# Expert stages of a fused transformer-and-state-space kernel: the slot tiles behind the sixteenth in nested conditional blocks

## The chip, the core and the metric

The kernel runs on one core of a Trainium2 chip. A core has five engines, each with its own instruction queue and its own sequencer: TensorE (PE: matrix products and transposes; its weight loads are listed as PEld), VectorE (DVE), ScalarE (ACT), GpSimd (POOL) and SyncE (SP, which here only issues transfers). Sixteen DMA engines move data between HBM and the on-chip memory. ACT, SP and POOL issue transfers. Engines wait for each other through semaphores.

The metric is the device time of one execution in microseconds (us). Before the change it is 2927.6 us, the median of three runs (2926.86 to 2928.7).

## The reference

One sequence of 1024 tokens of width 512 passes through two layers. Each part adds to the residual stream x:

```python
x = x + 0.5 * _L0_ffn_ref(_layernorm(x), ...)     # f0: 8 experts, top 2
x = x + _L0_attn_ref(_layernorm(x), ...)          # attention, 32 heads
x = x + 0.5 * _L0_ffn_ref(_layernorm(x), ...)     # f1: the same experts again
x = x + 0.5 * _L1_ffn_ref(_layernorm(x), ...)     # product with low-rank experts
x = x + _L1_attn_ref(_layernorm(x), ...)          # Mamba-like scan, 64 heads
x = x + 0.5 * _L1_ffn_ref(_layernorm(x), ...)
```

The part that the change touches is the first feed-forward network, which stands twice:

```python
logits = x @ W_gate + b_gate
_, top_idx = jax.lax.top_k(logits, 2)
y_all = jax.nn.relu(jnp.einsum('bsd,edh->bseh', x, W_e) + b_e)
y = jnp.take_along_axis(y_all, top_idx[..., None], axis=2)
return y.mean(axis=2)
```

Each token needs the outputs of two of eight experts, so 2048 rows in all go through some expert's 512x512 matrix.

## The kernel before

**The expert stage.** `expert_ffn(tag, ...)` runs twice, as f0 at the start and as f1 after the attention. It doesn't compute all eight experts for every token. It sorts the 2048 token-expert pairs into *slots*: each expert gets a whole number of tiles of 128 rows, at least one. The number of tiles in use depends on the data and lies between 16 (all counts multiples of 128) and 23. The program is laid out for the most, `NS = 2*S//P + NE - 1 = 23`, and always runs all 23. A tile behind the last one in use gathers token 0, multiplies it by the last expert's matrix, and stores rows that nobody reads.

**Routing.** VectorE computes from the gate's logits the two chosen experts of each token, the number of tiles of each expert (`nt`) and its running sum (`ends`; its last column is the number of tiles in use), the slot of each pair (`slot`), the token of each slot (`token`) and the expert of each tile (`of_i`).

**One slot tile** s then takes these steps.
- `gather(s)`: POOL issues an indirect transfer of 128 rows of the normalized input from the HBM buffer `rows` into a tile `xs` (three buffers).
- `turn(s)`: TensorE transposes it in four pieces (`ps_tr`, the helper's line L156), ACT copies the result to `xt_s` (three buffers, L494).
- Four products of 128x512 (`ps_e`, L527) with the expert's matrix, which is picked from `w_all` by a register that TensorE's sequencer loads from `of_i` (L523). Each product takes two passes.
- VectorE adds the expert's bias (`y_e`, L535, picked by a register of its own), ACT applies the relu and the factor 0.25 (L541) and issues the store of the tile to the HBM buffer `outs` (L542).

The loop runs one step ahead: `turn(s+1)` stands in front of the product of tile s, and gathers are issued two tiles ahead. A scheduler orders each engine's instructions at build time and places the waits.

**Work put between tiles.** `meanwhile` is a list of closures, one of which is run after every second tile from the fifth on. In f0 these load the first attention weights (`w_v`, `w_q`, `w_k`, `w_o`, SP queue) and then scale w_q (L676) and form sums of w_q and w_k on POOL (L653) for the first group of heads. In f1 they load and prepare weights of the second layer.

**Around the stage.** Before it, SP loads `w_all` (8 MB) and `b_all`. In f0 the first normalized tiles use a pool `own` of five buffers that is released after them. Behind it, `collect` issues two indirect gathers per token tile on POOL (`pair<-outs`, L555), VectorE adds them to x (L572), and a layer norm and the next stage's first products follow, tile by tile. The first collecting gather needs all stores to `outs`.

Of the kernel before, what the change touches and what calls it, by code (L numbers as in the profile page):

```python
# [13 lines left out]
F32 = mybir.dt.float32  # L14
BF16 = mybir.dt.bfloat16
I32 = mybir.dt.int32
# [6 lines left out]
P = 128  # L23
S = 1024
D = 512
NT = S // P
KT = D // P
# [6 lines left out]

NE = 8
NS = 2 * S // P + NE - 1
NE1 = 4
RANK = 8

# [36 lines left out]
def macaron_kernel(  # L76
# [23 lines left out]
    nc = tc.nc  # L100
# [8 lines left out]
    rows = dram.tile([S, D], F32, tag="rows", name="rows")  # L109
    outs = dram.tile([NS * P, D], F32, tag="outs", name="outs")  # L110

# [6 lines left out]
    x = const.tile([P, NT, D], F32, tag="x", name="x")  # L118
# [40 lines left out]
    def normalize(t, keep=False, pin=False, own=None):  # L159

        st = lnp.tile([P, 6], F32, tag="st", name="ln_st")
        nc.vector.bn_stats(st, x[:, t, :])
        mv = lnp.tile([P, 2], F32, tag="mv", name="ln_mv")
        nc.vector.bn_aggr(mv, st)
        rs = lnp.tile([P, 1], F32, tag="rs", name="ln_rs")
        root = rsqrt(rs, mv[:, 1:2], 1.0, EPS, 1)
        if pin:
            tc.keep_in_program_order(root)
        if own is None:
            xn = lnp.tile([P, D], F32, tag="xn", name="ln_xn")  # L170
        else:
            xn = own.tile([P, D], F32, tag="own", name="xn_own")
        nc.vector.tensor_scalar(xn, x[:, t, :], mv[:, 0:1], rs, ALU.subtract, ALU.mult)
        if keep:
            nc.scalar.dma_start(rows[t * P : (t + 1) * P, :], xn)
        normal[t] = xn
# [19 lines left out]
    def narrow_by_columns(t, w, n):  # L196

        ps = psml.tile([P, 512], F32, tag="ps", name="ps_nc")  # L200
        for k in range(KT):
            nc.tensor.matmul(
                ps[(k % 2) * MP : (k % 2) * MP + n, :P],
                lhsT=w[:, k, :n],
                rhs=hT[:, k, t * P : (t + 1) * P],
                start=(k < 2),
                stop=True,
                skip_group_check=k >= 2,
            )
        nt = halves[t % 2]  # L210
        if n == MP:
            nc.scalar.copy(nt, ps[:, :P])
        else:
            for i in range(2):
                nc.scalar.copy(nt[i * MP : i * MP + n, :], ps[i * MP : i * MP + n, :P])
        narrow[t] = nt
# [89 lines left out]
    def gate_steps(own=None):  # L306
        return (
            lambda t: normalize(t, True, own=own),
            transpose_h,
            None,  # L310
            lambda t: narrow_by_columns(t, gate_w, NE),
            gates,
        )

    def expert_ffn(tag, before_rows, meanwhile, behind_weights=lambda: None):
# [4 lines left out]

        with tc.tile_pool(name=f"{tag}wa", bufs=1) as wap, tc.tile_pool(
            name=f"{tag}r", bufs=1
        ) as rp, tc.tile_pool(name=f"{tag}w", bufs=3) as wk:
            w_all = wap.tile([P, NE, KT, D], F32, tag="w_all", name="w_all")
            b_all = wap.tile([P, NE, D], F32, tag="b_all", name="b_all")
            for e in range(NE):
# [3 lines left out]
                if e % 4 == 3:  # L330
                    for b in range(e - 3, e + 1):
                        nc.sync.dma_start(b_all[:, b, :], b_e[b].partition_broadcast(P))
            behind_weights()


            lanes = rp.tile([P, P], F32, tag="lanes", name="lanes")
            steps = rp.tile([P, NS + 1], F32, tag="steps", name="steps")
            counts = rp.tile([P, P], I32, tag="counts", name="counts")
            nc.gpsimd.iota(counts, pattern=[[1, P]], base=0, channel_multiplier=0)
            nc.gpsimd.tensor_copy(lanes, counts)  # L340
            nc.gpsimd.tensor_scalar(steps, lanes[:, : NS + 1], float(P), None, ALU.mult)
            lane = rp.tile([P, 1], F32, tag="lane", name="lane")
# [11 lines left out]
            nc.gpsimd.memset(going_on, 1.0)  # L354
            nc.gpsimd.memset(going_on[:, :, 0:1], 0.0)

            before_rows()
            sel1 = first_of_max(rp, lg, NE, "a")
            rest = rp.tile([P, NT, NE], F32, tag="rest", name="rest")
            nc.vector.scalar_tensor_tensor(rest, sel1, -3e38, lg, ALU.mult, ALU.add)  # L360
# [45 lines left out]
            ends = rp.tile([P, NE], F32, tag="ends", name="ends")  # L406
# [15 lines left out]
            for i, sel in enumerate((sel1, sel2)):  # L422
# [7 lines left out]
            flat = pos.rearrange("p i t -> p (i t)")  # L430
            past = rp.tile([P, n2, NS + 1], F32, tag="past", name="past_s")
            nc.vector.tensor_tensor(
                past,
                flat.unsqueeze(2).to_broadcast([P, n2, NS + 1]),
                steps.unsqueeze(1).to_broadcast([P, n2, NS + 1]),
                ALU.is_ge,
# [39 lines left out]
            gathered, turned = {}, {}  # L476

            def gather(s):
                xs = wk.tile([P, D], F32, tag="xs", name="xs")
                nc.gpsimd.indirect_dma_start(  # L480
                    out=xs,
                    out_offset=None,
                    in_=rows,
                    in_offset=bass.IndirectOffsetOnAxis(ap=token[:, s : s + 1], axis=0),
                    bounds_check=S - 1,
                    oob_is_err=True,
                )
                gathered[s] = xs

            def turn(s):  # L490
                xs = gathered.pop(s)
                ps = transposes(lambda i: xs[:, i * P : (i + 1) * P], KT)
                xt = wk.tile([P, KT, P], F32, tag="xt", name="xt_s")
                nc.scalar.copy(xt.rearrange("p k c -> p (k c)"), ps)  # L494
                turned[s] = xt

# [16 lines left out]
            for i in range(2):  # L513
                nc.vector.tensor_copy(slot[i], pos[:, i, :])
            turn(0)
            for s in range(NS):
                if s + 2 < NS:
                    gather(s + 2)
                if s + 1 < NS:
                    turn(s + 1)  # L520
                xt = turned.pop(s)
                low, high = max(0, s - (NS - NE)), min(s, NE - 1)
                ep = nc.tensor.value_load(of_i[0:1, s : s + 1], min_val=low, max_val=high)  # L523
                ev = nc.vector.value_load(of_i[0:1, s : s + 1], min_val=low, max_val=high)
                ps = psml.tile([P, 512], F32, tag="ps", name="ps_e")
                for k in range(KT):
                    nc.tensor.matmul(  # L527
                        ps,
                        lhsT=xt[:, k, :],
                        rhs=w_all[:, bass.ds(ep, 1), k, :].rearrange("p e c -> p (e c)"),  # L530
                        start=(k == 0),
                        stop=(k == KT - 1),
                    )
                y = wk.tile([P, D], F32, tag="y", name="y_e")
                nc.vector.tensor_tensor(  # L535
                    y,
                    ps,
                    b_all[:, bass.ds(ev, 1), :].rearrange("p e c -> p (e c)"),
                    ALU.add,
                )  # L540
                nc.scalar.activation(y, y, AF.Relu, scale=0.25)  # L541
                nc.scalar.dma_start(outs[s * P : (s + 1) * P, :], y)  # L542
                if s > 3 and s % 2 == 0 and meanwhile:
                    meanwhile.pop(0)()

    pairs = {}

# [27 lines left out]
    class Lora:  # L575


        def __init__(self, pool):
            self.store = False
            self.pool = pool  # L580
            self.nz = NE1 * RANK
            self.lg_w = pool.tile([P, KT, self.nz + NE1], F32, tag="lg_w", name="lg_w")
            nc.scalar.dma_start(self.lg_w, lora_gate_t.rearrange("(k p) c -> p k c", p=P))
            self.lb_w = pool.tile([self.nz, D], F32, tag="lb_w", name="lb_w")
            nc.scalar.dma_start(self.lb_w, lora_b)
            self.ebias = pool.tile([P, NE1], F32, tag="ebias", name="ebias")
            nc.scalar.dma_start(self.ebias, exp_bias.partition_broadcast(P))
# [5 lines left out]
        def gate(self, t):  # L593
            narrow_by_columns(t, self.lg_w, self.nz + NE1)

        def choose(self, t):
            nz = self.nz
            ps = narrow_by_rows(t, nz + NE1)
            lg = self.pool.tile([P, 1, NE1], F32, tag="lg", name="lg1")
            nc.vector.tensor_tensor(lg[:, 0, :], ps[:, nz : nz + NE1], self.ebias, ALU.add)  # L600
# [822 lines left out]
    with tc.tile_pool(name="left", bufs=1) as left:  # L1423
        first, later = {}, []
        causal = left.tile([P, P], F32, tag="causal", name="causal")
        make_causal_mask(nc, causal, mask_val=-1e30)

        def load_first():
            first.update(load_heads(0))
            first["left"] = left_of_heads(first, left, later)  # L1430

        later.append(load_first)

        def gates_of_input():
            with tc.tile_pool(name="own", bufs=5) as own:
                Tiles(*gate_steps(own)).flush()

        expert_ffn("f0", gates_of_input, later)
        attention(left, causal, first, Tiles(*gate_steps()))
    with tc.tile_pool(name="lora", bufs=1) as lp:  # L1440
        lora, par = Lora(lp), Scan(lp)
        expert_ffn("f1", lambda: None, [lora.load, par.ready, par.turn], par.load)
        mamba(lora, par)


# [49 lines left out]
```

## Time and profile before

| | |
|---|---|
| median of three runs | 2927.6 us |
| the profiled execution | 2928.29 us, of which its span 2926.6 us |
| granted TensorE clock, mean | 0.976 |
| f0: loop of slot tiles | first product 55.7 us, last pass ends 147.0 us |
| f1: loop of slot tiles | first product 1635.5 us, last pass ends 1725.8 us |
| products of both loops | 368 passes, 168.0 us busy |

The stretches around both loops, with the busy time of each engine, the granted clock of TensorE and the share of the DMA engines, read

```
0.00:46.50 46.50, 18.76 (x131) 12.41 (x131) 22.93 (x93) 9.97 (x25) 9.25 (x41) 0.80 0.98 346
46.50:60.00 13.50, 6.28 (x16) 3.45 (x17) 0.00 (x0) 1.17 (x2) 7.86 (x6) 0.57 0.88 288
60.00:147.10 87.10, 85.48 (x262) 41.51 (x260) 15.21 (x22) 24.14 (x43) 30.91 (x24) 1.00 0.42 124
147.10:187.00 39.90, 19.90 (x55) 10.02 (x56) 20.96 (x48) 5.13 (x10) 22.63 (x24) 0.70 0.39 112
1634.00:1726.00 92.00, 91.74 (x277) 44.95 (x275) 15.37 (x23) 25.50 (x46) 20.26 (x20) 0.98 0.42 122
```

(stretch and its length, then PE, PEld, VectorE, ACT and POOL busy us with the number of instructions, the granted clock, the DMA share and GB/s). In the profile, a line gives the engine, the source line, the operation with the tiles that it writes and reads, and in square brackets how long the engine had been idle and what ended that. "PEld", "PEq" or "PEldq" mark weight loads and TensorE's sequencer. In the chain of waits each piece is the work, or the wait, that the next one needed.

### The profile page before, as it was taken

The page shows a single profiled execution, that of the slowest core. Times are in us where ns is not written, and L with a number is a line of the kernel's source. Part 1 is how long each engine was busy: PE and PEld are TensorE (multiplying, and loading weights), DVE is VectorE, ACT ScalarE, POOL GpSimd, SP SyncE. Part 2 cuts the span into 40 slices and gives each one's busy share as a digit, 9 for nine tenths or more (in the row PEclk, how much of TensorE's full clock was granted, in tenths as well). Part 3 has the DMA queues.
Part 4 walks back from the last instruction along what each step waited for, and adds up shares of the span by engine and source line. Part 5 has one row for each costly group of instructions (what it writes and reads, how often), then busy time and mean ns, then how long its engine had stood idle before and what let it go on. Part 6 is the DMA issues. An engine that isn't in the chain of part 4 may idle for free.

```text
span 2926.6 us, 30414 instructions
## 1 busy us (share of the span) xinstructions
PE 2785.7 (95%) x11091; PEld 1578.9 (54%) x11091; DVE 1746.5 (60%) x3239; ACT 718.8 (25%) x1414; POOL 899.2 (31%) x737
## 2 busy tenths in 40 slices
PE   5979999999999999999999769899999999999998
PEld 3435666656666566666655334455555555555554
DVE  3146556565555655556555235677676777777673
ACT  2212212222212222212222223422222232222221
POOL 4231212121121211212200230255555545555451
PEclk7989999999999999999999889999999999999999
DMA  8421001010010001000015340233232222323210
GB/s 291 128 77 29 15 15 44 1 44 15 15 44 15 29 15 31 28 15 29 15 36 189 97 131 16 86 101 104 79 120 90 91 80 101 108 87 108 101 44 29
DMA packets 102180, 197.02 MB, mean 67 GB/s; under 512 B 9040, under 2 KB 34800, under 8 KB 102032
## 3 DMA queue, kind: packets, MB, share of 16 engines
q1 hardware_dynamic: 84896, 157.15, 16.3%
q0 software_dynamic: 6240, 20.45, 2.7%
q10 hardware_dynamic: 10896, 17.47, 1.6%
q8 instruction: 90, 1.47, 0.2%
q14 instruction: 58, 0.48, 0.1%
HBM read 176.17 MB, written 18.87 MB: 67 GB/s over the span
## 4 chain that ended last, share of the span: by engine, by line
PE 84%; DVE 6%; POOL 4%; DMA 3%; issue 3%; ACT 0%; SPq 0%; POOLq 0%; DVEq 0%; ACTq 0%
PE ps_in L247 15%; PE ps_m L929 13%; PE ps_o L749 8%; PE ps_s L725 8%; PE ps_tr L156 6%; PE ps_m L901 6%; PE ps_out L1377 6%; PE ps_wo L838 6%; PE ps_e L527 5%; PE ps_y L1325 3%; PE ps_up L258 2%; PE ps_st L1343 1%; DVE e_seg L1282 1%; DVE xc L1178 1%; PE ps_v L258 1%
## 5 line engine op out<-in xcount | busy, mean ns | idle before, releaser
L725 PE MATMUL ps_s<-kT,qT 128*128 128x512 f32 (+3 forms) x768 | 292.8, 488 | 0.1
L749 PE MATMUL ps_o<-pT,v 128*128 128x512 f32 (+3 forms) x768 | 258.6, 486 | 0.2 <-ACT pT L770 0.2
L770 ACT COPY pT<-ps_tr 128x256 f32<-128x256 f32 (+2 forms) x192 | 91.7, 477 | 646.5 <-PE ps_tr L156 635.0
L739 ACT ACTIVATE pr<-ps_s,nm 128x128 f32<-128x128 f32 (+7 forms) x256 | 190.3, 744 | 238.9 <-DVE nm L736 208.4
L1377 PE MATMUL ps_out<-w_out,yg 128*128 128x512 f32 x512 | 237.2, 606 | 2.0 <-DVE yg L1340 2.0
L247 PE MATMUL ps_in<-hT,w_g 128*128 128x512 f32 x512 | 226.7, 596 | 12.0 <-issue 12.0
L1307 POOL TENSOR_TENSOR cs<-cT,dd 128x1024 f32<-128x1024 f32 x56 | 181.7, 3245 | 163.8 <-PE ps_y L1325 139.4
L247 PE MATMUL ps_in<-hT,w_x 128*128 128x512 f32 x512 | 225.9, 593 | 0.0
L749 PEld LDWEIGHTS ps_o<-pT,v 128*128 128x128 f32 x768 | 143.5, 190 | 144.7 <-issue 98.8
L736 DVE TENSOR_REDUCE nm<-ps_s 128x1 f32<-128x128 f32 (+7 forms) x256 | 192.4, 753 | 3.9
L156 PEld LDWEIGHTS ps_tr<-ident,pr 128*128 128x128 f32 x1152 | 136.2, 141 | 76.4 <-issue 44.9
L156 PE MATMUL ps_tr<-ident,pr 128*128 128x128 f32 x1152 | 170.6, 275 | 4.4 <-DVE pr L741 3.2
L741 DVE TENSOR_SCALAR pr<-pr,sm 128x128 f32<-128x128 f32 (+7 forms) x256 | 163.8, 640 | 7.7 <-DVE sm L740 0.5
L527 PE MATMUL ps_e<-w_all,xt_s 128*128 (+1 forms) x368 | 168.0, 601 | 0.0
L247 PEld LDWEIGHTS ps_in<-hT,w_g 128*128 128x128 f32 x512 | 96.7, 190 | 132.1 <-issue 132.0
L247 PEld LDWEIGHTS ps_in<-hT,w_x 128*128 128x128 f32 x512 | 96.9, 190 | 120.4 <-issue 119.7
L1282 DVE TENSOR_TENSOR_SCAN e_seg<-dd,eye 128x1024 f32<-128x1024 f32 x64 | 153.9, 2404 | 8.2 <-PE ps_y L1325 6.1
L1178 DVE SCALAR_TENSOR_TENSOR xc<-ps_in,conv,xc 128x511 f32<-128x511 f32 (+2 forms) x192 | 141.6, 738 | 18.0 <-ACT xc L1174 17.6
L725 PEld LDWEIGHTS ps_s<-kT,qT 128*128 128x128 f32 x768 | 127.5, 192 | 39.8 <-issue 26.8
L1377 PEld LDWEIGHTS ps_out<-w_out,yg 128*128 128x128 f32 x512 | 93.0, 192 | 95.0 <-issue 94.6
L1301 POOL TENSOR_TENSOR xw<-xdt,erev 128x512 f32<-128x512 f32 x56 | 59.4, 1061 | 254.7 <-DVE xdt L1295 224.4
L823 POOL TENSOR_TENSOR so<-oT 128x256 f32<-128x256 f32 x28 | 20.1, 727 | 380.1 <-DVE oT L756 336.7
(274 smaller groups left out, 4760.5 us busy)
## 6 DMA issues: line engine op xcount, KB each, us to landing
dd<-decay SPq DMA_DIRECT2D x128, 512.0 KB
w_all<-in_w_e_dram SPq DMA_DIRECT2D x16, 1024.0 KB
outs<-y_e ACTq DMA_DIRECT2D x46, 256.0 KB
w_v<-in_wkv_dram SPq DMA_DIRECT2D x8, 1024.0 KB
w_q<-in_wq_dram SPq DMA_DIRECT2D x32, 256.0 KB
w_k<-in_wkv_dram SPq DMA_DIRECT2D x8, 1024.0 KB
w_o<-in_wo_dram SPq DMA_DIRECT2D x8, 1024.0 KB
w_x<-in_in_wt_dram SPq DMA_DIRECT2D x8, 1024.0 KB
```

What stands on the lines that cost most here:

```text
L156: nc.tensor.transpose(ps[:, i * P : (i + 1) * P], src(i), ident)
L247: nc.tensor.matmul(ps[:, cols : cols + n], lhsT=w[:, k, c0 : c0 + P], rhs=hT[:, k, t0 : t0 + n], start=(k == 0), stop=(k == KT - 1),)
L527: nc.tensor.matmul(ps, lhsT=xt[:, k, :], rhs=w_all[:, bass.ds(ep, 1), k, :].rearrange("p e c -> p (e c)"), start=(k == 0), stop=(k == KT - 1),
L725: nc.tensor.matmul(ps[:, j : j + m], lhsT=qT[:, qt * P : (qt + 1) * P], rhs=kT[:, j : j + m], start=True, stop=True,)
L736: nc.vector.tensor_reduce(nm, ps[:, :n], AX.X, ALU.max, negate=True)
L739: nc.scalar.activation(pr[:, :n], ps[:, :n], AF.Exp, bias=nm, accum_out=sm)
L749: nc.tensor.matmul(ps[:, lo:512], lhsT=v[:, kb, hh * P : (hh + 1) * P], rhs=pT[:, kb, lo:512], start=(kb == 0), stop=(kb == last),)
L838: nc.tensor.matmul(ps[:, j, :], lhsT=lf[i][k][:, j * P : (j + 1) * P], rhs=rt[i][:, k, :], start=(first and j == 0 and k == 0), stop=(k == 1),
L929: nc.tensor.matmul(ps, lhsT=gr["left"][i][:, k, hh * P : (hh + 1) * P], rhs=right[i][:, k, :], start=(first and k == 0), stop=(last and k ...
L1282: nc.vector.tensor_tensor_scan(e.rearrange("p h l -> p (h l)"), dd[:, 0, :], eye8.rearrange("p h l -> p (h l)"), 0.0, ALU.mult, ALU.add,)
L1307: nc.gpsimd.tensor_tensor(cs, un["cT"][:, tok].unsqueeze(1).to_broadcast([P, HPG, P]), dd[:, 1, :].rearrange("p (h l) -> p h l", l=P), ALU ...
L1377: nc.tensor.matmul(po, lhsT=yg[:, k, :], rhs=w_o[:, k, :], start=(k == 0), stop=(k == 3))
```

## The change

Tiles 0 to 15 run as before. Tiles 16 to 22 stand each inside a conditional block, and the blocks are nested: block s is entered if the number of tiles in use, n, is larger than s. When it is not, everything inside, so all later tiles, is left out. Four engines (PE, DVE, ACT and SP) load n into a register and compare it at each block; POOL has no instruction inside the blocks. In the built order each engine's blocks follow on one another, each opened by a compare-and-branch; the else parts and their jumps stand behind the last block. An else part waits for its engine's own work and brings its semaphores, and for SP those of the skipped stores, to the values that the skipped instructions would have left.

Five other things change with it.
- All gathers are issued outside the blocks. Those of tiles 16 to 18 use `xs` as before; those of 19 to 22 use a pool `more_rows` of five buffers, the one that held f0's first normalized tiles, which is now kept for the whole stage. In the built order of POOL these four stand right behind the gathers of tiles 2 to 4, and in f0 the scaling of w_q now stands behind the gather of tile 5.
- For tiles 16 and later the transposed rows are copied back into the gathered tile, not into `xt_s`.
- The register loads of `of_i` for tiles 16 to 22 stand inside the blocks.
- The work left in `meanwhile` is done before the first block.
- In f0 SP writes seven tiles of x to the rows of `outs` that belong to tiles 16 to 22, ahead of the attention weights. These rows then hold defined values also where no block stores.

```diff
+NS0 = 2 * S // P
...
             behind_weights()
+            if tag == "f0":
+                nc.sync.dma_start(
+                    outs[NS0 * P :, :].rearrange("(s p) c -> p s c", p=P), x[:, : NS - NS0, :]
+                )
...
             def gather(s):
-                xs = wk.tile([P, D], F32, tag="xs", name="xs")
+                if s < NS0 + 3:
+                    xs = wk.tile([P, D], F32, tag="xs", name="xs")
+                else:
+                    xs = more_rows.tile([P, D], F32, tag="own", name="xs_m")
...
             def turn(s):
...
-                xt = wk.tile([P, KT, P], F32, tag="xt", name="xt_s")
+                if s < NS0:
+                    xt = wk.tile([P, KT, P], F32, tag="xt", name="xt_s")
+                else:
+                    xt = xs.rearrange("p (k c) -> p k c", c=P)
...
             turn(0)
-            for s in range(NS):
-                if s + 2 < NS:
-                    gather(s + 2)
+            n_i = rp.tile([P, 1], I32, tag="n_i", name="n_i")
+            nc.vector.tensor_copy(n_i, ends[:, NE - 1 :])
+
+            def slot_tile(s):
                 if s + 1 < NS:
                     turn(s + 1)
...
                 nc.scalar.dma_start(outs[s * P : (s + 1) * P, :], y)
-                if s > 3 and s % 2 == 0 and meanwhile:
+
+            for s in range(NS0):
+                for i in range(s + 2, NS if s == NS0 - 2 else min(s + 3, NS)):
+                    if i not in gathered and i > 1:
+                        gather(i)
+                slot_tile(s)
+                if (s > 3 and s % 2 == 0) and meanwhile:
                     meanwhile.pop(0)()
+            while meanwhile:
+                meanwhile.pop(0)()
+
+            with ExitStack() as more_tiles:
+                n = nc.values_load(
+                    n_i[0:1, :],
+                    engines=[mybir.EngineType.PE, mybir.EngineType.DVE, mybir.EngineType.Activation, mybir.EngineType.SP],
+                    min_val=NS0,
+                    max_val=NS,
+                )
+                for s in range(NS0, NS):
+                    more_tiles.enter_context(tc.If(n > s))
+                    slot_tile(s)
```

More of the change, by code (lines that the diff above doesn't have):

```diff
@@ L322, in expert_ffn @@
             name=f"{tag}r", bufs=1
-        ) as rp, tc.tile_pool(name=f"{tag}w", bufs=3) as wk:
+        ) as rp, tc.tile_pool(name=f"{tag}m", bufs=5) as more_rows, tc.tile_pool(name=f"{tag}w", bufs=3) as wk:
             w_all = wap.tile([P, NE, KT, D], F32, tag="w_all", name="w_all")
@@ L355, in expert_ffn @@
             nc.gpsimd.memset(going_on[:, :, 0:1], 0.0)
-            before_rows()
+            before_rows(more_rows)
             sel1 = first_of_max(rp, lg, NE, "a")
@@ L1432, in macaron_kernel, with gates_of_input @@
         later.append(load_first)
-        def gates_of_input():
-            with tc.tile_pool(name="own", bufs=5) as own:
-                Tiles(*gate_steps(own)).flush()
+        def gates_of_input(own):
+            Tiles(*gate_steps(own)).flush()
         expert_ffn("f0", gates_of_input, later)
@@ L1441, in macaron_kernel @@
         lora, par = Lora(lp), Scan(lp)
-        expert_ffn("f1", lambda: None, [lora.load, par.ready, par.turn], par.load)
+        expert_ffn("f1", lambda own: None, [lora.load, par.ready, par.turn], par.load)
         mamba(lora, par)
```

## The prediction

> **What bounds the kernel now.** I read the page first, then the chain of waits around the first expert stage (0 to 200 us), then the timeline of both stages by engine, then the rows of single tiles. The two expert stages (called f0 and f1 in the code) are the only places that the change touches: after I take away buffer numbers and line numbers, the built order of the changed kernel has the same instructions in the same order on every engine outside them.
>
> ```profile
> span 2926.6 us, 30414 instructions
> PE 2785.7 (95%) x11091; PEld 1578.9 (54%) x11091; DVE 1746.5 (60%) x3239; ACT 718.8 (25%) x1414; POOL 899.2 (31%) x737
> L527 PE MATMUL ps_e<-w_all,xt_s 128*128 (+1 forms) x368 | 168.0, 601 | 0.0
> ```
>
> TensorE is busy for 95% of the span, and the expert product (L527) runs 368 times: two stages of 23 slot tiles, 8 passes each. It never waits (0.0).
>
> ```profile
> 135.83 0.44 PE ps_tr L156 x4
> 136.27 3.44 PE ps_e L527 x8
> 139.70 0.44 PE ps_tr L156 x4
> 140.14 6.88 PE ps_e L527 x16
> 147.10 0.70 DVE y_e L535
> 147.83 0.64 ACT y_e L541
> 148.49 2.00 DMA outs<-y_e
> 150.55 0.49 issue
> 151.26 0.34 POOL pair L555
> ```
>
> This is the chain of waits in f0 (start, duration, engine, tile, line). A slot tile costs the chain 0.44 + 3.44 = 3.87 us, all TensorE: the four transposes of the next tile, then this tile's eight passes. The last tile has no transposes to make and costs 3.44. Behind it stands a tail that any last tile leaves: bias on VectorE, relu, the store, its landing, the first collecting gather, 4.2 us from 147.02 to 151.26. f1 has the same period, and its first collecting gather starts 4.4 us after its last pass (1725.75 to 1730.19). So what is taken off the number of tiles comes off the span at TensorE's price, if nothing else becomes late.
>
> ```profile
> L527 PEldq EVENT_SEMAPHORE  x46: 51/51/3560, 54.8 to 1715.4; - x46
> L523 PEldq TENSOR_LOAD <-of_i x23: 295/299/812, 1621.2 to 1716.1; - x23
> 1714.66 0.69 DVE L535 TENSOR_TENSOR y_e<-ps_e,b_all 128x512 f32<-128x512 f32 x1 [3.18 <-PE ps_e L527]
> 1718.71 7.03 PE L527 MATMUL ps_e<-w_all,xt_s 128*128 x16
> ```
>
> These are rows of TensorE's sequencer (the first from the product's line, the second from the tile of_i in f1; durations are min/median/max) and two of f1's timeline. The sequencer waits at 1715.4 for VectorE's y of two tiles ago (1714.66 + 0.69), then issues a whole tile in 0.7 us (its next row, a register load for the last tile, is at 1716.1), while the array starts that tile at 1718.71. It is 3.3 us ahead of the array. And the register loads of f1 stand between its tiles (the built order has the last five there), where the period is still 3.87 us: one load costs the array nothing.
>
> **The change part by part.** I evaluated the reference's routing on its own inputs (seed 0). The counts per expert are 248 221 241 282 295 279 237 245 in f0, which makes 19 tiles of 128 in use, and 269 225 255 258 296 258 225 262 in f1, which makes 21. So 4 and 2 of the 23 tiles are skipped.
>
> *Removed.* f0: three tiles of 3.87 and the last one's 3.44, 15.05 us; f1: 3.87 + 3.44 = 7.31 us. Together -22.4 us. The transposes of the first unused tile (19 in f0, 21 in f1) are still made in the block before, and are counted in its 3.87.
>
> *The blocks.* f0 runs three blocks and leaves at the fourth compare; f1 runs five and leaves at the sixth. In each, TensorE's sequencer gets a compare and a register load of of_i with two register operations (before they were mostly done ahead of the loop). The load is 0.30 us by its row; the compare has no row. The nearest are the register operations (0.05 us each), so 0.4 to 0.5 us per block; the lead of 3.3 us hides it, and without that lead 8 blocks would cost 8 x 0.5 = 4 us. VectorE idles 3.18 us per tile and ScalarE 2.76, which hides theirs. Value taken 0; bounds 0 and +4. [...]
>
> *The exits.* Each engine jumps to an else part that waits for its own work and adds what the skipped tiles would have added to its semaphores. Behind it, TensorE's first work waits 16.5 us anyway (transposes at 163.48), ScalarE's 16.2 us, VectorE's 6.9 us. SyncE adds for the skipped stores: it waits for older stores of the same semaphores (by the built order none younger than tile 14's in f0), so it is through before the last store lands. POOL's first gather now waits also for TensorE's addition, which comes 4 us before the landing. I take 0.5 us per stage, +1.0; bounds 0 and, if each exit cost as much as a whole DMA round (2.0 us, the row of the store), +4.
>
> *The fill.* In f0 SyncE writes 7 tiles of x (1.84 MB) to the unused rows of outs, behind the last bias row and ahead of w_v, w_q, w_k, w_o. By the DMA view of 20 to 70 us the engines are full and move about 390 GB/s until 55, so this is 1.84 / 0.39 = 4.7 us of their time. Late next is not a weight (w_v is used at 169, w_q is scaled at 56 before and later now) but the first gathers: the one issued at 46.78 is transposed at 53.72, 6.9 us later; in f1, with idle DMA, 1628.89 to 1633.61, 4.7 us. If the queues share, the gather is slowed no more than now (0); if the backlog is served in order, by the bytes that stand ahead. Each transfer waits for the one eight before it, so the fill replaces w_k in what is outstanding at 46.8: 0.79 MB more, 2 us. Bounds 0 and +4.7, value +1.5.
>
> *POOL's order.* The gathers of tiles 19 to 22 now stand early (two behind the third gather, in the 4.4 us that POOL idles at 50.7; one each behind the next two), and the scaling of w_q moves behind the sixth gather. Now there is a stall in f0:
>
> ```profile
> 71.51 2.36 POOL L653 TENSOR_TENSOR sqk<-w_q,sqk 128x1024 f32<-128x1024 f32 x1
> 74.03 1.04 POOL L480 DMA_INDIRECT xs<-rows,token  x1 [0.16 <-issue]
> 77.55 0.63 PE L156 MATMUL ps_tr<-ident,xs 128*128 128x128 f32 x4 [1.53 <-DMA xs<-rows,token]
> ```
>
> Three sums hold the seventh gather until 74.03, and its rows come 1.53 us late. In the new order that gather stands behind two scalings (2 x 2.78) after the sixth (61.3 + 1.1): it issues at about 68.0, needs 3.5 us, and is there well before 75.9. The eighth stands behind three sums: 68.0 + 1.1 + 3 x 2.36 = 76.2, there at 79.7, needed at 79.75. So the stall shrinks to 0 to 0.5. Value -1.2; bounds -1.5 and +1.
>
> *Sum* against the profiled execution (2928.3 us, span 2926.6): 2928.3 - 22.4 + 0 + 1.0 + 1.5 - 1.2 = 2907.2. It lies 0.7 above the median of the runs (2927.6), so 2906.5 to 2907.2; I say 2907.
>
> **The rivals.**
>
> *Every compare fetches instructions.* The page's instruction queue q8 moved 1.47 MB in 90 packets, 0.2% of 16 engines' span: 0.002 x 16 x 2926.6 / 90 = 1.0 us a packet; with a round like the store's 2.0 us a fetch is about 3 us. TensorE's lead of 3.3 us just covers it. ScalarE does 0.59 + 0.63 + 0.33 = 1.55 us of a tile's 3.87; 3.0 more makes 4.55, so 8 blocks lose 0.7 each, 5.5 us, and the exits (two jumps in f0, three in f1, on VectorE against 6.9) 9.0 - 6.9 = 2.1. Time 2907 + 7.6 = 2915. For it: nothing here has ever branched inside the program. Against it: a used block follows straight on in the built order, and the jump is over some 130 instructions at most. [...]
>
> *The lead is lost*: the sequencer can't run ahead over a compare, and each block pays its loads, the four issues and the first weight load with an idle array, about 1 us by the 0.7 us that issuing a tile takes and the 0.3 of the load: 8 x 1 = 8, 2915 too.
>
> *Slower: each block is a barrier.* If a block starts only when the tile before has been stored, as the stage's end does, it pays the tail of 4.2 us: 8 x 4.2 = 34, so 2907 + 34 = 2941. It decides from 22.4 / 8 = 2.8 us per block. For it: at the stage's end just this wait is seen. Against it: the built order shows no barrier at a compare, its waits there are on the routing's count alone, and the next tile's transposes still stand ahead of a tile's product.
>
> *The gain is given back at the start*: fill served wholly first and the gathers behind it, +4.7, with the stall kept (+1.2) and exits at +4, blocks +4: 2907 + 3.2 + 1.2 + 3 + 4 = 2918, still faster.
>
> *It doesn't skip as counted*: another rounding on the chip moves a count over 256 (f1 has 255 and 258): 3.87 us either way, 2903 or 2911; it is held in the forecast's own range.
>
> **How the numbers follow.** Forecast as summed (2903 to 2911) 0.71; fetches or lost lead (2911 to 2918) 0.13; start and exits at their bounds 0.04; barrier 0.07; another cost of branches that just eats the gain, with no place that I can name, 0.05. The range 2903 to 2917 leaves out the barrier, the nameless cost and the ends of the rest. About 0.2%, 5.9 us, is what a measurement of this kernel can tell from no change, so faster means below 2921.7: 0.71 + 0.13 + 0.04 = 0.88; same 0.05; slower 0.07.
>
> **What would show it.** Right: the product's line with 184 + 184 - 48 = 320 passes; 19 and 21 tiles at a period of 3.87 us through the 17th and later; 4.2 to 5 us from the last pass to the first collecting gather; f0's first product within 0 to 3 us of 55.7; the stall at the seventh tile gone. Wrong: gaps of TensorE in front of each tile from the 17th (lead lost above 0.5 us, fetch on ScalarE if y waits there, barrier at 4 us); VectorE's first sum in x later than 7.6 us behind the last y; the first product of f0 later than 59; or 368 passes.

## The result, and the profile after

The changed kernel takes 2904.7 us, the median of five runs (2902.9 to 2907.5), against 2927.6 us for the kernel before (five runs, 2925.7 to 2930.5). The ratio is 0.9921, with a 95% interval of 0.9907 to 0.9936. The change makes the kernel faster by 22.9 us; 2907 was predicted. The profiled execution has a span of 2903.0 us at a granted clock of 0.977, so in the two profiles the span is shorter by 23.6 us.

From the page of the changed kernel, the busy times:

```profile
PE 2761.5 (95%) x11027; PEld 1567.6 (54%) x11027; DVE 1741.1 (60%) x3235; ACT 713.1 (25%) x1404; POOL 898.6 (31%) x737
```

TensorE is busy for 24.2 us less (2785.7 to 2761.5), which is the whole gain and a little more. It executes 64 matrix instructions fewer: six tiles of eight passes, 48, and four transposes for each of four tiles. (Tiles 19 and 21 are still turned, by the block ahead of them.) The queue that carries instructions moves as many packets as before, 90. The rows of the product's line, now L540, say the same:

```profile
L540 PE MATMUL ps_e<-w_all,xt_s x256: 592/592/1061, 55.6 to 1681.9; 128*128 x120, 128*128 128x512 f32 x8
L540 PE MATMUL ps_e<-w_all,xs x48: 592/592/595, 120.4 to 1693.5; 128*128 x48
L540 PE MATMUL ps_e<-w_all,xs_m x16: 592/592/595, 1694.4 to 1701.3; 128*128 x16
```

256 + 48 + 16 passes make 320 in place of 368. The columns behind the count are the shortest, median and longest duration in ns and the first and last start in us. The last two `xs_m` tiles are those of f1, whose 20th and 21st tile stand in the fourth and fifth block.

The end of f0 on the timeline: VectorE's y of the last tile, ACT's store of it, and the first collecting gather (start, duration, engine, line, operation; in brackets the idle time ahead and what ended it):

```profile
131.85 0.69 DVE L548 TENSOR_TENSOR y_e<-ps_e,b_all 128x512 f32<-128x512 f32 x1 [3.18 <-PEq L567]
...
133.24 0.33 ACTq L555 DMA_DIRECT2D outs<-y_e  x1
136.31 1.01 POOL L587 DMA_INDIRECT pair<-outs,slot_i  x1 [22.20 <-issue]
```

It has the shape of the chain before, 15.25 us earlier: the last y starts at 131.85 in place of 147.10. VectorE still idles 3.18 us ahead of each y, so the blocks run at the old period. In the weight loads of this stage the transposes start at 119.98, 123.85 and 127.73, which is 3.87 us apart.

The ledger of the two profiled executions, by the starts of these rows:

| stretch (us) | before | after | difference |
|---|---|---|---|
| start to f0's first gather | 46.78 | 46.58 | -0.20 |
| f0: first gather to last y | 100.32 | 85.27 | -15.05 |
| f0: last y to first collecting gather | 4.16 | 4.46 | +0.30 |
| to f1's first gather (attention within) | 1477.63 | 1477.22 | -0.41 |
| f1: first gather to last y | 96.95 | 88.44 | -8.51 |
| f1: last y to first collecting gather | 4.35 | 4.60 | +0.25 |
| to the end of the span | 1196.4 | 1196.4 | 0.0 |

The time comes out of the two stages and nowhere else.

### The profile page after: what moved, and what is told of

Same layout as the page of the kernel before. It is cut to its first block, busy times and chain, and to the rows that moved or that the text cites. A ratio compares the mean times of both kernels' runs of the same rounds, so it can differ in the third digit from the quotient of the medians.

```text
span 2903.0 us, 30288 instructions
## 1 busy us (share of the span) xinstructions
PE 2761.5 (95%) x11027; PEld 1567.6 (54%) x11027; DVE 1741.1 (60%) x3235; ACT 713.1 (25%) x1404; POOL 898.6 (31%) x737
## 5 line engine op out<-in xcount | busy, mean ns | idle before, releaser
L708 POOL TENSOR_SCALAR w_q<-w_q 128x1024 f32<-128x1024 f32 x16 | 44.6, 2785 | 292.1 <-DMA w_q<-in_wq_dram 291.6
```

## The experiments

Two theories stood against each other from the start. *A*: the gain is the number of skipped tiles times TensorE's 3.87 us, and blocks, exits and fill cost next to nothing, since they lie beside other work. *B*: each block costs the array something (a lost lead or a fetch), which is made up elsewhere. A third, *C*, had part of the gain from the moved gathers rather than from the count. All times below are medians, with ratios to the kernel before in the same rounds. In the first four runs that kernel stood at 2929.4 us, in the last four at 2926.35.

### All 23 tiles through the blocks

```diff
-            nc.vector.tensor_copy(n_i, ends[:, NE - 1 :])
+            nc.vector.tensor_scalar(n_i, ends[:, NE - 1 :], 0.0, 23.0, ALU.mult, ALU.add)
```

> The changed kernel with its count of tiles fixed at 23, so that every block runs and no else part does: all 23 tiles of both stages are computed, 14 blocks are entered. Theory A (the gain is skipped tiles at TensorE's 3.87 us each, blocks cost nothing because the sequencer runs ahead): the 22.4 us come back whole, 2904.7 + 22.4 = 2927.1, less up to 1.1 for the two exits that are gone, so 2926.0 to 2927.1, within 1.6 us of the kernel before (2927.6). Rival B (a block costs the array something, 0.5 us or more, made up elsewhere): 14 blocks x 0.5 = 7 us, 2933 or more, with gaps on TensorE ahead of tiles 16 to 22. Rival C (several us of the gain come from the gathers' new order or another thing than the count): 2923 or less.

Measured: 2933.8 us, ratio 1.0014 (1.0005 to 1.0023), 4.4 us slower than the kernel before. That is the number of rival B, but not its place. TensorE has no gaps ahead of tiles 16 to 22: y follows y in 3.87 us through all blocks. What is late is ACT. Its timeline in f0:

```profile
135.94 0.63 ACT L554 ACTIVATE y_e<-y_e 128x512 f32<-128x512 f32 x1 [2.20 <-DVE y_e L548]
...
137.03 0.59 ACT L506 COPY xs_m<-ps_tr 128x512 f32<-128x512 f32 x1 [0.46 <-ACT y_e L554]
139.47 0.58 ACT L506 COPY xs_m<-ps_tr 128x512 f32<-128x512 f32 x1 [1.85 <-PE ps_tr L157]
147.12 0.63 ACT L554 ACTIVATE y_e<-y_e 128x512 f32<-128x512 f32 x1 [7.07 <-DVE y_e L548]
...
148.37 0.63 ACT L554 ACTIVATE y_e<-y_e 128x512 f32<-128x512 f32 x1 [0.62 <-ACT y_e L554]
...
149.61 0.63 ACT L554 ACTIVATE y_e<-y_e 128x512 f32<-128x512 f32 x1 [0.61 <-ACT y_e L554]
150.27 0.33 ACTq L555 DMA_DIRECT2D outs<-y_e  x1
```

Up to tile 19 a relu stands every 3.87 us. Then two copies follow each other without a relu between them, and the relus and stores of tiles 20, 21 and 22 come in a row behind the last y (146.40). In the built order of ACT the inner block stands ahead of the relu of the outer tile: copy, compare, copy, compare, relu and store of tile 22, jump, relu and store of tile 21, jump, relu and store of tile 20. Two pairs of 1.24 us (147.12 to 148.37 to 149.61) stand ahead of the last store, so the first collecting gather is at 153.09, 6.69 us behind the last y; in f1 it is 7.09. Against 4.16 and 4.35 these are 5.3 us. The stages themselves are a little shorter than before (99.38 and 96.63 us from first gather to last y against 100.32 and 96.95). So the count carries the gain, but the nested form has a price when 22 or 23 tiles are in use, which this input (19 and 21) doesn't pay.

### No blocks at all

```diff
-            with ExitStack() as more_tiles:
...
-                for s in range(NS0, NS):
-                    more_tiles.enter_context(tc.If(n > s))
-                    slot_tile(s)
+            for s in range(NS0, {"f0": 19, "f1": 21}[tag]):
+                slot_tile(s)
```

> The changed kernel with the blocks replaced by plain loops over 19 tiles in the first stage and 21 in the second, the counts in use: no compare, no load of the count, no else part. Theory A: 2904.7 less the exits' 0.55 (their tails measured 4.46 and 4.60 us against 4.16 and 4.35), so 2904.1 to 2904.7, no difference that can be measured. Rival B (a compare costs the array its lead, 0.5 to 1 us per block, 8 blocks): 2896.7 to 2900.7.

Measured: 2909.2 us, ratio 0.9932 (0.9918 to 0.9945); the interval overlaps that of the change. Rival B's 2897 to 2901 falls. The tails are 4.47 and 4.56 us, as with the blocks, so the 0.25 and 0.30 us that they are longer than before aren't the price of the exits. It isn't a hair faster than the change, as was expected, but looks slower by some 3 us. The profile has a place for that, in f0:

```profile
82.49 1.08 PE L157 MATMUL ps_tr<-ident,xs 128*128 128x128 f32 x4 [2.53 <-DMA xs<-rows,token]
83.37 4.64 PE L540 MATMUL ps_e<-w_all,xt_s 128*128 x8
```

Without the blocks the planner put the eighth gather behind all four of POOL's sums, at 79.03 us. Its rows are 2.53 us late, and the tile after it ran slowly (1.08 for 0.60 and 4.64 for 3.60 us): together y came 8.04 us behind y, a loss of 4.17 us, where the changed kernel loses 1.56 in its profile. The slow tile is TensorE's clock: the granted clock is 1.00 from 79 to 82 us, 0.51 from 82 to 84 and 0.64 from 84 to 86. Behind the waits of 1.53 us (before) and 0.84 us (the changed kernel) it stayed at 1.00. A further 0.7 us stands at the start of f1, where 17 register loads precede the first transposes in place of the changed kernel's 16 (below).

### Twice the fill

```diff
+    spare = dram.tile([(NS - NS0) * P, D], F32, tag="spare", name="spare")
...
+                nc.sync.dma_start(
+                    spare.rearrange("(s p) c -> p s c", p=P), x[:, : NS - NS0, :]
+                )
```

> The changed kernel with the fill's traffic doubled: right behind the fill, SyncE writes the same 1.84 MB of x once more, into rows that nothing reads. Theory A (the fill is free, since queues share the DMA engines and the first gathers are served beside it): first product of the first stage at 55.6 to 56, time 2904.7 to 2906, the rest being a longer stall at a later gather. Rival (the fill is served ahead of the gathers, 1.84 MB at about 390 GB/s): 4.7 us more for the second copy if not for the first, 2909.4, with the first gathers landing later by that much.

Measured: 2907.2 us, ratio 0.9927 (0.9913 to 0.9940), not to be told from the change. But two effects cancel in it. The first gather is at 48.67 us and the first product at 57.40, 1.8 us later than in the profile of the changed kernel and 0.7 to 1.8 later than in the eight profiles with one fill. The gathers are not what got slower: from first gather to first product it is 8.73 us against 9.00. The steps of the routing ahead of it did, 21.65 us from the last copy of the gate's transposes to the first gather against 20.1 to 20.9 in the eight profiles with one fill and 19.97 in the single one with none. Why they take longer beside the transfer wasn't tried. On the other side the planner, with w_q due later, put the eighth gather ahead of the sums, and f0 loses only 0.3 us at one tile. So the second copy costs 0.8 to 1.5 us at the start, and the first one 0.2 to 0.9.

### No tile behind the sixteenth

```diff
+            nc.vector.tensor_scalar(n_i, ends[:, NE - 1 :], 0.0, 16.0, ALU.mult, ALU.add)
```

(in place of the same line as in the first experiment)

> The changed kernel with its count fixed at 16, so that every block is skipped at the first compare: tiles 16 to 18 of the first stage and 16 to 20 of the second, whose rows are in use, are left out. Theory A: eight more tiles of 3.87 us go, 2904.7 - 31.0 = 2873.7, within 1.5 us. Rival D (an else part costs by the number of tiles that it stands for, or the gathers and sums on POOL end the first stage once it is shorter): 2 to 4 us above that, 2876 to 2878, with a tail longer than the 4.5 us between last pass and first collecting gather.

Measured: 2875.2 us, ratio 0.9815 (0.9801 to 0.9828). Against the change's ratio that is 0.0106 x 2929.4 = 31 us less, theory A's eight tiles of 3.87. The tails are 4.30 and 4.63 us: skipping all seven tiles by one else part costs no more than skipping two or four, and POOL doesn't become the end of the stage.

### The change once more, and a fourth buffer for the gathered rows

> The changed kernel, unaltered, once more beside the runs that follow, because the kernel before stood at 2929.4 us in the first four runs and at 2927.6 when the change was measured. Expected ratio to the kernel before: 0.9921 as then, within 0.0015, so about 23 us less than the kernel before in the same rounds.

Measured: 2905.6 us (2903.7 to 2906.8), ratio 0.9925 (0.9912 to 0.9938), as before.

```diff
-        ) as rp, ... tc.tile_pool(name=f"{tag}m", bufs=5) as more_rows, tc.tile_pool(name=f"{tag}w", bufs=3) as wk:
+        ) as rp, ... tc.tile_pool(name=f"{tag}x", bufs=4) as xsp, tc.tile_pool(name=f"{tag}t", bufs=2) as xtp, ...
...
-                    xs = wk.tile([P, D], F32, tag="xs", name="xs")
+                    xs = xsp.tile([P, D], F32, tag="xs", name="xs")
...
-                    xt = wk.tile([P, KT, P], F32, tag="xt", name="xt_s")
+                    xt = xtp.tile([P, KT, P], F32, tag="xt", name="xt_s")
```

> The changed kernel with four buffers in place of three for the gathered rows (and two in place of three for the turned rows), so that each gather may go one tile earlier. The order on POOL is the same, gathers 7 to 9 still stand behind scalings and sums, but what they fetch is needed 3.87 us later. Theory A (the first stage's 1.56 us of waiting for gathered rows at tiles 7 and 8 are due to gathers that are one tile too close): no such wait, 1.5 us less than the changed kernel in the same rounds. Rival (the gathers' landing sets the pace, whatever the buffers): the waits stay, no difference. Rival (two buffers for the turned rows are too few): gaps of TensorE at every tile, slower by some 0.1 us a tile, 4 us.

The changed kernel first, TensorE in f0 where POOL's sums hold the gathers up:

```profile
80.70 0.63 PE L157 MATMUL ps_tr<-ident,xs 128*128 128x128 f32 x4 [0.84 <-DMA xs<-rows,token]
...
85.10 0.63 PE L157 MATMUL ps_tr<-ident,xs 128*128 128x128 f32 x4 [0.33 <-DMA xs<-rows,token]
```

and the same stretch with four buffers:

```profile
80.81 0.60 PE L157 MATMUL ps_tr<-ident,xs 128*128 128x128 f32 x4
...
84.68 0.60 PE L157 MATMUL ps_tr<-ident,xs 128*128 128x128 f32 x4
```

The waits are gone (a row without brackets had no idle time ahead), and no new gap has come from the two buffers of `xt_s`. f0 takes 84.14 us from first gather to last y, against 85.27 and 85.58 in the two profiles of the changed kernel. Measured: 2903.3 us (2902.5 to 2905.7), ratio 0.9920 (0.9907 to 0.9933), 2.3 us less than the changed kernel in the same rounds. The two sets of six runs overlap, so the median speaks for it and the profile shows its cause, but the runs alone don't settle its size. Of the versions that compute every tile in use it has the lowest median, but by its ratio it can't be told from the change (0.9921).

### The blocks one after another

```diff
-                    more_tiles.enter_context(tc.If(n > s))
-                    slot_tile(s)
+                    with tc.If(n > s):
+                        slot_tile(s)
```

> The changed kernel with its seven blocks one after another, not nested. By the built order each block that runs then ends in a jump past its else part, four blocks of the first stage and two of the second are skipped one by one, each through an else part of its own, and the relu and store of tile 15 stand behind all blocks on ScalarE. Theory A (jumps of about 0.05 us lie under TensorE's lead; what costs is work that the built order puts behind the blocks): period 3.87 as before, about 1.25 us more per stage for one more relu and store behind the last tile (0.63 + 0.33 us and the gaps around them, as in the run with all blocks), and 0.5 us for the skipped else parts, 2 to 4 us more than the changed kernel. Rival B (each taken jump empties what the sequencer had run ahead): 8 blocks with 0.5 us or more of gap on TensorE, 4 us more in the periods themselves.

Measured: 2913.95 us, ratio 0.9952 (0.9938 to 0.9965), 8.3 us slower than the nested form. Now there are gaps inside the blocks, 4.56 us from y to y in place of 3.87, as rival B would have them. VectorE and TensorE in f0:

```profile
124.92 0.60 PE L157 MATMUL ps_tr<-ident,xs 128*128 128x128 f32 x4
125.18 0.69 DVE L548 TENSOR_TENSOR y_e<-ps_e,b_all 128x512 f32<-128x512 f32 x1 [3.18 <-PE ps_e L540]
125.97 3.67 PE L540 MATMUL ps_e<-w_all,xs 128*128 x8 [0.45 <-issue]
```

and the product's line at TensorE's sequencer, cut to the stretch of the second block:

```profile
L540 PEldq EVENT_SEMAPHORE  x1: 4848/4848/4848, 121.1 to 121.1; - x1
```

But the jump isn't what makes them, though compares and jumps take 0.07 to 0.35 us on TensorE's sequencer, where 0.05 was expected of a jump. The transposes behind the jump start on time (124.92, 3.87 us behind the ones before), so the sequencer had run ahead over the block's end. Then it waits from 121.1 for 4.85 us, until 125.95, and the product starts at 125.97: that is the end of VectorE's y of the tile just before (125.18 + 0.69 = 125.87). In the nested form the product waits for the y of the tile before that one, which is long done. So the price of a block of its own, 0.69 us, is VectorE's y: the wait placed behind a closed block is one tile stricter. f0 has two such boundaries and f1 four (4.56 to 4.61), 4.2 us in all. The tails are 6.74 and 5.98 us against 4.45 and 4.59 in the changed kernel of the same rounds, 3.7 us more, with the relu and the store of tile 15 standing behind the blocks. In f0 ACT first goes through the four skipped blocks, from 136.03 to 137.47 us, more than the 0.5 us that was expected for them. 4.2 + 3.7 = 7.9 of the 8.3.

> The blocks one after another and the count fixed at 23, so that all of them run: against the nested blocks with 23 (4.4 us slower than the kernel before) this takes away only the nesting. Theory A (in the nested blocks the relu and store of tiles 20, 21 and 22 stand behind the innermost block on ScalarE, so the last store goes out 2 x 1.25 us late in each stage, tails 6.7 and 7.1 us against 4.2 and 4.4): here only tile 15's relu and store stand there, so at most 1.25 us per stage remain and the time is 1 to 2.5 us less than with the nested blocks. Rival (the 5.3 us are the price of leaving seven blocks, by jumps): as slow as nested or slower.

Measured: 2940.8 us, ratio 1.0046 (1.0033 to 1.0060), 9 us slower than the nested blocks with 23 by the two ratios. The tails shrink as theory A had it, from 6.69 and 7.09 to 5.71 and 5.49 us, 2.6 together. It was still wrong about the time, since it had not foreseen the stricter wait: at five of the six boundaries per stage y now follows y in 4.56 us and more (at the last, where no transposes follow, in 3.62 and 3.76 in place of 3.43), and the stages 104.36 and 98.98 us from first gather to last y against 99.38 and 96.63. That is 7.3 more and 2.6 less, 4.7 us. The two profiled spans differ by 6.7; 2.5 of that lie behind f1's first collecting gather, in a part that the edit doesn't touch. There the granted clock differs: it stands at half for 66.7 us in this profile and for 58.8 to 61.2 us in the nine others, whose stretch takes 1195.5 to 1197.8 us against 1199.95 here.

## Why the prediction came out

**The tiles, -22.4: right.** 320 passes, 19 and 21 tiles at 3.87 us. f0's stage lost 15.05 us where 15.05 was summed. f1's lost 8.51 where 7.31 was summed; the 1.2 more are the start of the stage. From f1's first gather to its second y it took 15.68 us in the profile of before and 14.53 after. Most of this is a term that the prediction put at nothing. TensorE's sequencer works through register loads of `of_i` before it issues f1's first transposes, and the change moved two of them into the blocks. Before, and then in the changed kernel (the loads that stand ahead, and the first transposes):

```profile
L523 PEldq TENSOR_LOAD <-of_i x18: 295/299/307, 1621.2 to 1632.9; - x18
1633.61 1.96 PE L156 MATMUL ps_tr<-ident,xs 128*128 128x128 f32 x8 [5.92 <-issue]
```

```profile
L536 PEldq TENSOR_LOAD <-of_i x16: 294/299/309, 1606.2 to 1616.6; - x16
1617.33 2.35 PE L157 MATMUL ps_tr<-ident,xs 128*128 128x128 f32 x8 [5.18 <-DMA xs<-rows,token]
```

The loads start some 0.7 us apart. Before, TensorE waits for no rows there (`issue`), and the transposes follow the last load. They start 4.72 us behind f1's first gather before, 4.55 in the static loop with 17 loads, and 3.80 to 3.84 in the eight profiles with 16: 0.9 us of the gain. The prediction's "one load costs the array nothing" holds between the tiles, where it was read, and not at the start of f1. The other 0.2, and the spread of this stretch over 13.8 to 15.6 us in the experiments, are for the most part the moment at which TensorE's clock comes back (below): from the first transposes to the second y the ten profiles took 10.0 to 11.8 us, and the shorter the sooner the clock was full, 3.0 to 6.4 us behind these transposes. The runs with 16 and with 23 tiles fix the price from both sides: 31 us for eight tiles fewer, and no gain left with all of them.

**The blocks, 0: right, and for the reason given.** The rows of the compares and jumps (L567) on two of the four engines that have them:

```profile
L567 PEldq COMPARE_BRANCH  x12: 72/76/357, 114.3 to 1702.2; - x12
L567 ACTq COMPARE_BRANCH  x12: 34/34/50, 122.5 to 1703.7; - x12
```

TensorE's sequencer does its first one at 114.3 us, while the array starts that tile's transposes at 119.98: it is 5.7 us ahead, more than the 3.3 of the prediction, which was read at another point of the loop. At all eight compares that enter a block it is 3.9 to 6.1 us ahead. A compare takes 0.08 us and a register load with its register operations some 0.7 us (1.2 in f0's first block), more than the 0.4 to 0.5 us of the prediction; nothing of it reaches the array. The rivals of a fetch at each compare and of the lost lead have no gap to stand in, and the static loop didn't beat the blocks. The barrier rival (4.2 us per block) falls with the period. The fetches show nowhere: 90 instruction packets before and after.

In rows that hold the compares and the jumps at the exits together, the medians are 76 ns on TensorE's sequencer, 45 on VectorE's and 34 to 36 on the two others. On TensorE's the eight compares that enter a block take 72 to 93 ns, and those that leave and the jumps 174 to 357. The prediction had put a compare at the 50 ns of a register operation; the lead covers the difference.

**The exits, +1.0: too high.** The tails are longer by 0.30 and 0.25 us, and they are so in the static loop, which has no exits (4.47 and 4.56). What was put down to them is 0, the lower bound. The last store lands 3.4 us behind the last y before and after. What is longer is POOL's row of semaphore waits behind the landing, four in place of one in f0 and six in place of three in f1, 0.09 us apart: 0.27 us more in each stage.

**The fill, +1.5: too high.** The first product came at 55.58 us in place of 55.73, and in the seven other profiles with one fill at 55.7 to 56.7, so the term lies between 0 and 1 us. The part on the gathers came out at its lower bound: they are served no later (9.00 us from first gather to first product, 8.95 before). From 51.3 to 54 us their queue moves 0.55 MB while the queue of SP's transfers moves 0.36; before, it was 0.52 beside 0.52. Of the two cases that were named, sharing is the one that fits; the backlog in order would have moved that stretch by the prediction's 2 us, and even the second fill left it at 8.73. What a second fill costs, 0.8 to 1.5 us, it costs ahead of the gathers, a place that the prediction didn't name.

**POOL's order, -1.2: wrong in what it said, and small.** The step that failed is "the stall shrinks to 0 to 0.5". The gathers and sums of the changed kernel on POOL, in f0:

```profile
68.18 1.09 POOL L489 DMA_INDIRECT xs<-rows,token  x1 [0.27 <-issue]
...
74.11 2.35 POOL L685 TENSOR_TENSOR w_k<-w_q,w_k 128x1024 f32<-128x1024 f32 x1
76.60 1.03 POOL L489 DMA_INDIRECT xs<-rows,token  x1
77.67 2.36 POOL L685 TENSOR_TENSOR sqk<-w_q,sqk 128x1024 f32<-128x1024 f32 x1
80.19 1.04 POOL L489 DMA_INDIRECT xs<-rows,token  x1 [0.16 <-issue]
```

The issues came where the sum put them (68.18 for 68.0, 76.60 for 76.2), and the gather at 68.18 is on time. But the next two were 0.84 and 0.33 us late: rows asked for at 76.60 were turned at 80.70, 4.1 us later, where 3.5 was reckoned, and the last one, behind one more sum, wasn't looked at. So the stall moved by one and two tiles. It cost 1.56 us in this profile and 0.84 in the second one of the same kernel, against 1.69 before. The fourth buffer shows that it was only a matter of how early a gather may go.

The three mis-sized terms sum to +1.3 (1.0 + 1.5 - 1.2) where the ledger has +0.2 (tails +0.55, start -0.20, stall -0.13). That is 1.1 too much; with the 1.2 at f1's start and the 0.4 between the stages it explains, within 0.2, how 2907.2 became 2904.7 against the profiled execution. That the total came so near is partly luck: the mis-sized terms offset each other in part, one was left out, and the restart of the clock alone moves single profiles by about 1 us.

## What to carry to other kernels

The skipped work was worth its time on the engine that bounds the stage, 31 us for eight tiles of 3.87 us on TensorE, and the conditional blocks cost that engine nothing: its sequencer ran 3.9 to 6.1 us ahead, and the compare and the register loads took 0.8 to 1.3 us of that. At the start of f1, where it had no lead, the same register loads did count: with two fewer ahead of them, the first transposes started 0.9 us sooner. What a block did cost was in what the planner put around it, so read the built order: nested, it put the ends of the outer tiles (relu and store) behind the inner blocks, 2.5 us of tail per stage once all blocks run; one after another, it made each product wait for the tile just before, 0.69 us per block. A change in one place also re-deals a planner's other queues: the position of one gather among four sums was worth between 0.3 and 4.2 us in these runs, up to more than a whole tile.

## What the runs showed of the hardware

After the pause between f0 and the attention TensorE's clock comes back at different times in the same program. Two profiles of the changed kernel over the same stretch (window and its length, TensorE's busy time, the granted clock, the DMA share, GB/s):

```profile
152.00:154.00 2.00, 1.01 (x5) 0.50 0.54 162
...
156.00:158.00 2.00, 2.00 (x4) 0.70 0.54 141
158.00:160.00 2.00, 2.00 (x9) 1.00 0.58 174
```

```profile
152.00:154.00 2.00, 0.42 (x2) 0.50 0.67 211
...
156.00:158.00 2.00, 2.00 (x4) 0.50 0.50 135
158.00:160.00 2.00, 2.00 (x5) 0.63 0.56 145
```

Continuous work begins at about 153.0 in the first and 153.6 in the second. In the first the clock is full from 157.2 (0.70 is the mean of half the rate for 1.2 us and the full rate for 0.8), 4.2 us later; in the second from 159.5, 5.9 us later. From the next stage's first transposes to the first copy of v the ten profiles took 10.7 to 11.8 us. The edits don't touch this stretch, so some 1 us varies there from profile to profile, and a difference of one or two microseconds between single profiles can't be told from it.
